# An approximate-matmul residual block on one NeuronCore: indirect writes, weight preparation and a norm placed at other steps

## The chip, the cores and the metric

The kernel runs on one core of a Trainium2 chip. The metric is the device time of one execution in microseconds, taken as the median of several executions. All data is fp32.

## What is computed

The input `x` has 16 samples of 256 channels of 28 x 28 pixels. Each sample is group-normalised (32 groups of 8 channels), goes through two "approximate matmul" 3 x 3 convolutions with a batch norm each, a squeeze-and-excite gate, and two residual additions:

```python
def amm_conv3x3(x, centroids, w_sub, stride=1):
    patches = jax.lax.conv_general_dilated_patches(x, (3, 3), ...)
    p = patches.reshape(B, C, s, Ho * Wo).transpose(0, 3, 1, 2)
    d = jnp.sum(p * p, -1)[..., None] - 2.0 * jnp.einsum('bncs,cks->bnck', p, centroids) + ...
    attn = jax.nn.softmax(-d, axis=-1)
    lut = jnp.einsum('cks,cso->cko', centroids, w_sub)
    out = jnp.einsum('bnck,cko->bno', attn, lut)
...
out = amm_conv3x3(x, centroids1, wsub1)
out = relu(bn_inference(out, ...))
out = amm_conv3x3(out, centroids2, wsub2)
out = se_layer(bn_inference(out, ...), ...)
return x0 + relu(out + x)     # x = group norm of x0
...
```

For every channel and pixel, the 9 patch values are compared with 16 centroids, a softmax over these 16 gives weights, and the weighted centroids times `w_sub` are summed over all 256 channels and 9 taps.

## The kernel before, in words

The program is one long unrolled list. It goes through 32 samples: 16 samples of layer 1 (numbers 0 to 15), then the same 16 of layer 2 (16 to 31). Each sample is four blocks: two halves of the channels (`hh`) by two halves of the image (14 rows, 392 pixels). A block takes two steps, so a sample takes 8 steps and the whole program some 256 and a tail. "Step 6.3" below means step 3 of sample 6, which is number 8 x 6 + 3 = 51 in the code.

The order is written out by hand. `at(cl, sub, f, ...)` (line 843) files a call under the step `cl` and a place `sub` in it; at line 1040 all calls are made in the order of `(cl, sub)`. Every engine then executes its own instructions in just this order. A place in the list is thus a place in each of the queues that the call uses: TensorE (PE), VectorE (DVE), ScalarE (ACT), GpSimd (POOL) and SyncE (SP, which issues most DMAs). An instruction that waits holds up all that is behind it on its engine.

One step of TensorE holds, in this order:

- sub 0.1 and 0.2, `logits` (line 357): patches times centroids, 32 x 32 tiles, 64 records in the trace. They read `pt`, the patches, which SP loads from the DRAM scratch `home1` or `home2` two steps ahead (`patches`, sub 0.5). ACT then makes exponentials (`exps`, line 369).
- in even steps sub 1.3 `num_b` (line 418) and 1.35 `num_a` (line 404): sums of exponentials, and numerators. In odd steps `num_a` alone, at 1.0.
- sub 2.0, `product` (line 486, tile `acc`): the normalised weights `q` times the weight matrices, mostly 18 records of 340 ns. This is the lookup and sum over channels. One of eight products falls in each step; step 6 has a short one.

The softmax's division: DVE makes a reciprocal, spreads it over partitions (`spread`, tiles `rb`), and GpSimd multiplies (`scale_q`, line 467: at sub 1.71 for the ninth tap in even steps, twice at 1.8 in odd steps). The products are arranged in the manner of Strassen's scheme: GpSimd also subtracts whole `q` buffers (`mix`, line 495), so a product may wait for a GpSimd that is late. Mixes stand at sub 2.5 of steps 5 and 7, 1.75 and 2.6 of step 7, and 1.0 of step 2.

Work around this that the change touches:

- `to_home2` (line 549): when a sample of layer 1 is finished, its two channel halves (`o`), each in two shifted copies (`r`), are written to `home2[b]` by indirect DMAs that GpSimd issues. Rows go to places given by an index tile `col`, since layer 2 uses its channels in another order. There are four writes per sample. They go to the same tensor, so each waits until the one before has landed. In sample 0 the order isn't known yet; its output is kept in DRAM (`d_h0`) and written later from a stage buffer (`h0_load`, `h0_put`).
- the order of channels: `rank_make` on DVE, `rank_look` (an indirect read, line 616), `rank_cols`.
- preparation of layer 2's weights during layer 1: `codes_load/put` and `sub_load/put` load centroids and `w_sub` into the stage buffer and scatter their rows by indirect writes (line 629); `prep_wd0` to `prep_wd4` lay out and centre the centroids (`center_sq` on GpSimd, line 259, gives `sq`; `center_add` has a matmul `sqp`, line 264, that reads it, and a DVE add); `prep_cw*` make the matrices of the numerators; `sums_load/put` make sums of weight matrices in five pieces. The stage buffer `st` (tag "pb") exists once, so each of these waits for the one before to be read out.
- `norm_out` (line 532): the batch norm of one quarter of a sample, on ACT. In layer 2 it also sums its output (`accum_out`) for the gate; `se_hidden` (line 752) multiplies these sums on TensorE.
- `gn_mean` (line 295): group statistics of the next input sample.

Of the kernel before, what the change touches and what calls it, by code (L numbers as in the profile page):

```python
# [8 lines left out]
F32 = mybir.dt.float32  # L9
I32 = mybir.dt.int32  # L10
U32 = mybir.dt.uint32
AF = mybir.ActivationFunctionType
# [5 lines left out]
P = 128  # L18
# [7 lines left out]
K = 16  # L26
S = 9
# [40 lines left out]
def kernel(  # L68
# [20 lines left out]
    nc = tc.nc  # L89
    B, C, _ = x.shape  # L90
    NB = C // P
# [4 lines left out]
    small = ctx.enter_context(tc.tile_pool(name="small", bufs=2))  # L96
# [144 lines left out]
    bn = []  # L241
# [53 lines left out]
    def gn_mean(b, k0=0, n=NB):  # L295
        st, mv = gst[b]
        ps = bank("gnp")[:, : 2 * n]
        nc.tensor.matmul(
            ps, lhsT=gmat, rhs=mv[:, k0 : k0 + n].rearrange("p b t -> p (b t)"), start=True, stop=True
        )  # L300
        gm = small.tile([P, NB, 2], F32, name="gn_gm")
        nc.vector.tensor_copy(gm[:, :n].rearrange("p b t -> p (b t)"), ps)
        dv = small.tile([P, NB], F32, name="gn_dv")
        nc.vector.tensor_sub(dv[:, :n], mv[:, k0 : k0 + n, 0], gm[:, :n, 0])
        nc.vector.tensor_mul(dv[:, :n], dv[:, :n], dv[:, :n])
        gst[b, "m"] = gm, dv

# [189 lines left out]
    ys = {}  # L497
# [34 lines left out]
    def norm_out(l, b, o, t, src=None):  # L532
# [5 lines left out]
        else:  # L538
# [4 lines left out]
                accum_out=ys[b, "sum"][:, o, t : t + 1],  # L543
            )

    idx = {}

    def to_home2(b, o, r, src=None):
        nc.gpsimd.indirect_dma_start(
            out=home2[b].rearrange("c u n -> (c u) n"),  # L550
            out_offset=bass.IndirectOffsetOnAxis(ap=idx["col", o, 5 + r][:, 0:1], axis=0),
            in_=(hpads[o] if src is None else src)[:, r : r + HROW], in_offset=None,
        )
# [74 lines left out]
    def scatter(dst, col, o, src):  # L628
        nc.gpsimd.indirect_dma_start(
            out=dst, out_offset=bass.IndirectOffsetOnAxis(ap=idx["col", o, col][:, 0:1], axis=0),  # L630
            in_=src, in_offset=None,
        )

    pw = {}
# [5 lines left out]
    def h0_load(o):  # L640
        nc.sync.dma_start(stage()[:, :NPAD], d_h0[o * P : (o + 1) * P, :])

    def h0_put(o):
        for r in range(2):
            to_home2(0, o, r, pw["st"])

    def codes_load(o):
        st = stage()
        nc.sync.dma_start(st[:, : S * K], sk2[o * P : (o + 1) * P, :])
        nc.sync.dma_start(st[:, 256 : 256 + S * K], ks2[o * P : (o + 1) * P, :])  # L650

    def codes_put(o):
        st = pw["st"]
        scatter(d_sk, 0, o, st[:, : S * K])
        scatter(d_ks, 1, o, st[:, 256 : 256 + S * K])

    def sub_load(o, part):
        n = 4 * C if part < 2 else C
# [93 lines left out]
    def se_hidden(b):  # L752
        ysum = ys[b, "sum"]
        ps = bank("sep")[: 2 * RED, :1]
        n = 0
        for k in range(NB):
            for i in range(2):
                nc.tensor.matmul(  # L758
                    ps, lhsT=w1_sb[:, k, :], rhs=ysum[:, k, i : i + 1],
                    start=(n == 0), stop=(n == 2 * NB - 1),  # L760
                )
                n += 1
        hid = small.tile([2 * RED, 1], F32, name="se_hid")
        nc.scalar.activation(hid, ps, AF.Relu, bias=b1_sb, scale=1.0 / HW)
        se[b] = small.tile([2 * RED, NB], F32, name="se_hh")
        nc.scalar.activation(se[b], halves, AF.Copy, scale=hid)
# [76 lines left out]
    def at(cl, sub, f, *a, **kw):  # L843
        jobs.setdefault((cl, sub), []).append((f, a, kw))
# [20 lines left out]
    for j, u in enumerate(blocks):  # L865
        g = 2 * j
        u["w"] = j
        wide = u["l"] == 1 and u["hh"] == 0
        for p in range(2):
            u["pt", p] = pts[p]  # L870
            at(g + p - NPT, 0.5, patches, u, p, nc.gpsimd if 0 < g + p < 5 else None)
            for q in range(2):
                mm = 2 * p + q
                at(g + p, 0.1 + 0.1 * q, logits, u, mm)
                if wide and mm == 0:
                    at(g, 0.12, wide_copy, u, mm)
                    at(g, 0.9, wide_turn, u, mm)
                    at(g, 0.95, wide_sub, u, mm)
                    at(g + 1, 0.3, wide_back, u, mm)
                    at(g + 1, 0.9, wide_exp, u, mm)  # L880
                else:
                    at(g + p, 0.12 + 0.1 * q, exps, u, mm)
        at(g + 2, 1.3, num_b, u)
        at(g + 2, 1.4, split_b, u)
        at(g + 2, 1.5, join_b, u)
        at(g + 2, 1.6, recip_dve, u)
        at(g + 2, 1.7, spread, u, 4)
        at(g + 2, 1.71, scale_q, u, 4)
        for mm in range(2):
            at(g + 2, 1.35, num_a, u, mm)  # L890
            at(g + 2, 1.45, copy_a, u, mm)
            at(g + 3, 1.8, spread, u, mm)
            at(g + 3, 1.8, scale_q, u, mm)
        for mm in range(2, 4):
            at(*((g + 2, 1.8) if mm == 2 else (g + 3, 0.05)), spread, u, mm)
            at(g + 3, 1.0, num_a, u, mm)
            at(g + 3, 1.1, scale_a, u, mm)

    for l in range(2):
        for b in range(B):  # L900
# [17 lines left out]
            at(g + 10, 0.05, reg_add, l, b, c12, c22, None)  # L918
            at(g + 10, 0.06, reg_add, l, b, c22, c21, None)
            at(g + 11, 0.0, acc_add, l, b, c12, (n, 10))  # L920
            at(g + 11, 1.9, norm_out, l, b, *c12)
            at(g + 11, 1.91, norm_out, l, b, *c22)
            at(g + 12, 0.0, acc_add, l, b, c11, (n, 11))
            at(g + 12, 0.3, norm_out, l, b, *c11)
            at(g + 13, 0.0, acc_add, l, b, c21, (n, 12), op=ALU.subtract)
            at(g + 13, 0.3, norm_out, l, b, *c21)
            if l == 0:
                for o in range(2):
                    if b == 0:
                        at(g + 12 + o, 0.35, rank_score, o)  # L930
                        at(g + 12 + o, 0.6, rank_keep, o)
                        at(g + 12 + 2 * o, 0.65, h0_keep, o)
                    else:
                        for r in range(2):
                            at(g + 12 + o + (o and r), (0.5, 2.9)[r] if o == 0 else (2.4, 2.9)[r], to_home2, b, o, r)
                if b + 1 < B:
                    at(*((g - 1, 2.6) if b else (2, 1.65)), load_x, b + 1)
                    for q in range(NB):
                        at(g + (1 + q if b else 4), 0.3, gn_stats, b + 1, q)
                    at(g + (3 if b else 4), 2.1, gn_mean, b + 1)  # L940
                    at(g + 4, 2.1 if b else 2.2, gn_var, b + 1)
                    for q in range(NB):
                        at(g + 5, 0.9 if b else 0.3, gn_apply, b + 1, q)
                        at(g + 5, 1.9 if b or q else 0.9, to_home1, b + 1, q)
            else:
                last = b == B - 1
                at(*((g + 11, 0.6) if last else (g + 13, 2.6)), load_x, b, last)
                at(g + 13, 2.1, se_hidden, b)
                at(g + 14, 1.05 if last else 2.1, se_gate, b)
                for q in range(NB):  # L950
                    at(*((g + 12, 0.4) if last else (g + 19, 0.9)), finish_norm, b, q)
                    if not last:
                        at(g + 19, 0.91, finish_gate, b, q)
                        at(g + 20, 0.05, finish_sum, b, q)
                        at(g + 20, 0.9, finish_relu, b, q)
                        at(g + 21, 0.05, finish_add, b, q)
                        at(g + 21, 0.06, store, b, q)
                    else:
                        at(g + 14, 1.92, finish_fast, b, q)
                        at(g + 14, 1.92, store, b, q)  # L960
                if b == B - 1:
                    at(g + 11, 0.65, flags)
                    at(g + 12, 2.9, flag_sum)
# [12 lines left out]
    at(14, 0.7, rank_row)  # L976
    for o in range(2):
        at(15 + o, 1.9, rank_make, o)
        at(16 + o, 2.7, rank_look, o)
    for o in range(2):  # L980
        at(18 + o, 2.7, rank_cols, o)
        at(20 + 2 * o, 0.6, h0_load, o)
        at(21 + 2 * o, 2.7, h0_put, o)
        at(24 + 2 * o, 0.6, codes_load, o)
        at(25 + 2 * o, 2.7, codes_put, o)
        for part in range(3):
            c = 28 + 6 * o + 2 * part
            at(c, 0.6, sub_load, o, part)
            at(c + 1, 2.7, sub_put, o, part)
    at(41, 0.6, prep_wd0)  # L990
    at(43, 0.3, prep_wd1)
    for part in range(3):
        at(43 + 2 * part, 1.9, prep_wd2, part)
        at(44 + 2 * part, 1.05, prep_wd3, part)
    at(51, 1.9, prep_wd4)
    at(52, 0.6, prep_cw0)
    at(53, 1.9, prep_cwa)
    for part in range(4):
        at((59, 60, 67, 68)[part], 2.3, prep_cwb, part)
    at(92, 2.3, load_se)  # L1000
    for n in range(5):
        at(70 + 2 * n, 0.6, sums_load, 2 * n)
        at(71 + 2 * n, 2.3, sums_put, 2 * n)
    g = 8 * B
    at(g - 2, 0.4, load_wd, 1, 0)
    at(g, 0.4, load_wd, 1, 1)
# [190 lines left out]
```

## Time and profile before

| | |
|---|---|
| median of 3 runs | 2750.07 us (2749.22 to 2758.3) |
| profiled execution | 2756.05 us |
| its span, first to last instruction | 2754.6 us |
| granted TensorE clock | 0.993 |
| indirect writes to `home2` (line 549) | 64, each 1.0 us of GpSimd |
| 392-column norm of layer 2 (line 541) | 64, median 763 ns, and 250 ns to read the sum |
| subtraction or product of a pair on GpSimd | 128 x 784, 1.86 us |
| layer 2's norm of the input (line 790) | 128 x 784, median 1096 ns |
| landing of a `home2` write after its issue | 3.2 to 8.4 us, median 5.8 |

The profile is of one execution. A line of its groups or timeline gives start and duration in us, engine, line of the code, operation, output and inputs, shape, count, and in brackets the idle time of the engine just before with what ended it. A matmul's end is modelled. A group of matmuls that overlap has a length from its first start to its last end, not a sum.

### The profile page before, as it was taken

To read this page: it belongs to the slowest core of one execution; us is meant where nothing else is said; L and a number is where in the kernel's file an instruction comes from. 1 tells how busy PE (TensorE), PEld (TensorE's weight loads), DVE (VectorE), ACT (ScalarE), POOL (GpSimd) and SP (SyncE) were. 2 spreads that over 40 slices of the span, in tenths; PEclk is the share of its full clock that TensorE was granted. 3 is DMA by queue.
4 is the path that set the end of the run, shared out by engine and by line. 5 is a ranking of instruction groups with operands and counts; after the bars stand their busy time and mean duration, and the time that the engine had idled before them with its cause. 6 is when DMAs were issued, how large, how long until landed. Compare 5 with 4: busy or idle time off the path is not lost.

```text
span 2754.6 us, 87978 instructions
## 1 busy us (share of the span) xinstructions
PE 2684.1 (97%) x37044; PEld 1298.7 (47%) x37044; DVE 1717.0 (62%) x3943; ACT 1461.7 (53%) x3293; POOL 2076.5 (75%) x1425
## 2 busy tenths in 40 slices
PE   5899999999999999999999999999999999999998
PEld 2444444444444444444444444444444444444444
DVE  4765555566655565555477666676666676766674
ACT  3445455444545444555455566665566565566553
POOL 3856787767887667766678687888787779787787
PEclk9999999999999999999999999999999999999999
DMA  9675676655677656655585555545555545555442
GB/s 195 149 141 145 157 188 183 163 118 146 153 184 186 156 120 157 165 157 148 116 184 123 112 117 119 111 100 118 123 122 119 113 101 116 119 124 119 109 106 60
DMA packets 223626, 374.53 MB, mean 136 GB/s; under 512 B 30633, under 2 KB 194009, under 8 KB 223225
## 3 DMA queue, kind: packets, MB, share of 16 engines
q1 hardware_dynamic: 216280, 334.87, 53.7%
q0 software_dynamic: 6944, 33.95, 3.6%
q8 instruction: 296, 4.85, 0.8%
q14 instruction: 106, 0.86, 0.1%
HBM read 288.93 MB, written 79.80 MB: 134 GB/s over the span
## 4 chain that ended last, share of the span: by engine, by line
PE 89%; DMA 3%; POOL 3%; SPq 1%; issue 1%; DVE 1%; ACT 1%; ACTq 0%; POOLq 0%; DVEq 0%
PE acc L486 47%; PE lg L357 17%; PE na L404 12%; PE nb L418 12%; DMA pt<-home 2%; POOL qp L495 2%; DMA home<-xpad 1%; SPq L343 1%; POOL qp L467 1%; SPq L347 1%; DMA row<-in_before 0%; ACT e L369 0%; POOL qo L493 0%; PE sep L758 0%; PE sep L770 0%
## 5 line engine op out<-in xcount | busy, mean ns | idle before, releaser
L369 ACT ACTIVATE e<-lg 128x392 f32<-128x392 f32 x1920 | 779.9, 524 | 795.4 <-PE lg L357 793.5
L495 POOL TENSOR_TENSOR qp<-qp,qp 128x784 f32<-128x784 f32 x512 | 939.0, 1864 | 21.5 <-DVE qp L478 21.5
L486 PE MATMUL acc<-qp,w_S 128*128 128x392 f32 x2048 | 706.6, 495 | 3.9 <-POOL qp L495 3.7
L467 POOL TENSOR_TENSOR qp<-qp,rb 128x784 f32<-128x784 f32 x256 | 470.1, 1857 | 209.4 <-DVE rb L459 201.3
L357 PE MATMUL lg<-pt,wd 32*32 32x392 f32 x16384 | 555.9, 503 | 19.7 <-DMA pt<-home 15.0
L459 DVE STREAM_SHUFFLE rb<-r 128x392 f32<-128x392 f32 x1024 | 550.9, 603 | 0.0
L486 PEld LDWEIGHTS acc<-qp,w_S 128*128 128x128 f32 x2048 | 386.8, 190 | 304.0 <-issue 15.7
L486 PE MATMUL acc<-qp,w_A 128*128 128x392 f32 x1536 | 521.3, 492 | 0.0
L438 DVE SCALAR_TENSOR_TENSOR r<-nb,kst,r 128x392 f32<-128x392 f32 x128 | 79.8, 623 | 570.9 <-ACT r L429 547.0
L404 PE MATMUL na<-e,cwa 64*32 64x392 f32 x8192 | 410.5, 496 | 8.5 <-issue 6.2
L486 PEld LDWEIGHTS acc<-qp,w_A 128*128 128x128 f32 x1536 | 291.8, 190 | 213.8
L418 PE MATMUL nb<-e,cwb 64*32 64x392 f32 x8192 | 374.9, 499 | 2.6 <-issue 2.1
L357 PEld LDWEIGHTS lg<-pt,wd 32*32 32x32 f32 x16384 | 236.3, 103 | 266.8 <-issue 184.7
L444 DVE RECIPROCAL r<-r 128x392 f32<-128x392 f32 x128 | 331.8, 2592 | 0.0
L467 POOL TENSOR_TENSOR qo<-qo,rb 128x392 f32<-128x392 f32 x128 | 131.1, 1024 | 247.8 <-DVE rb L455 247.6
L478 DVE TENSOR_TENSOR qp<-na,rb 128x392 f32<-128x392 f32 x512 | 252.5, 554 | 71.2 <-PE na L404 68.0
L404 PEld LDWEIGHTS na<-e,cwa 64*32 64x32 f32 x8192 | 146.9, 106 | 237.2 <-ACT e L369 119.9
L418 PEld LDWEIGHTS nb<-e,cwb 64*32 64x32 f32 x8192 | 143.8, 108 | 225.3 <-issue 140.8
L472 ACT COPY qp<-na 128x392 f32<-128x392 f32 x512 | 212.4, 513 | 12.0 <-PE na L404 10.2
L429 ACT ACTIVATE r<-nb,kst 128x392 f32<-128x392 f32 x128 | 87.7, 685 | 115.0 <-PE nb L418 111.2
L493 POOL TENSOR_TENSOR qo<-qo,qo 128x392 f32<-128x392 f32 x128 | 130.9, 1023 | 2.2
L375 ACT COPY e<-lg 128x392 f32<-128x392 f32 x128 | 52.9, 500 | 149.8 <-PE lg L357 149.8
(147 smaller groups left out, 1769.7 us busy)
## 6 DMA issues: line engine op xcount, KB each, us to landing
pt<-home SPq DMA_DIRECT2D x768, 209.0 KB
pt<-home SPq DMA_DIRECT2D x756, 104.5 KB
home<-xpad SPq DMA_DIRECT2D x31, 899.0 KB
xt<-in_x SPq DMA_DIRECT2D x30, 784.0 KB
out_dram<-y SPq DMA_DIRECT2D x32, 392.0 KB
w_S<-d_wS SPq DMA_DIRECT2D x4, 576.0 KB
st<-in_wsub SPq DMA_DIRECT2D x4, 512.0 KB
st<-d_wa SPq DMA_DIRECT2D x16, 128.0 KB
```

Source lines behind the costliest of these rows:

```text
L357: nc.tensor.matmul(bk[32 * c : 32 * c + 32, :N].rearrange("p (r w) -> p r w", w=W), lhsT=wts["wd", u["hh"]][32 * i : 32 * i + 32, mm, c, : ...
L369: nc.scalar.activation(eg[:, i, :], bk[:, :N], AF.Exp, scale=2.0)
L404: nc.tensor.matmul(bs[r][32 * i : 32 * i + 32, :N], lhsT=wts["cwa", u["hh"]][64 * r : 64 * r + 64, mm, i, :], rhs=es[64 * r : 64 * r + 64, ...
L418: nc.tensor.matmul(bs[r][32 * i : 32 * i + 32, :N], lhsT=wts["cwb", u["hh"]][64 * r : 64 * r + 64, mm, i, :], rhs=es[64 * r : 64 * r + 64, ...
L444: nc.vector.reciprocal(u["r"], u["r"])
L459: nc.vector.stream_shuffle(rb[:, r, :], u["r"], mask_of(2 * mm + r))
L467: nc.gpsimd.tensor_tensor(q, q, u.pop(("rb", mm)), ALU.mult)
L472: nc.scalar.copy(u["q", 2 * mm + r], bk[:, :N])
L478: nc.vector.tensor_mul(u["q", 2 * mm + r], bk[:, :N], rb[:, r, :])
L486: nc.tensor.matmul(accs[key][:, :N], lhsT=wl[w][:, k, :], rhs=us["q", k], start=first and n == 0, stop=last and n == len(ks) - 1,)
L493: nc.gpsimd.tensor_tensor(out_u["q", 8], in0["q", 8], in1["q", 8], ALU.subtract)
L495: nc.gpsimd.tensor_tensor(pair(out_u, mm), pair(in0, mm), pair(in1, mm), ALU.subtract)
```

## The change

- Layer 1's `to_home2` writes: (o=0, r=0) goes from sub 0.5 to 1.72 of step 12 of its sample's schedule (step 4 of the sample after), behind `scale_q` 4; (o=1, r=0) goes from 2.4 to 1.805 one step later, between the two calls of `scale_q`, for which these are now filed at 1.8 and 1.81. The two with r=1 stay at 2.9.
- `rank_look` for both halves goes to step 17, sub 1.805.
- The writes of sample 0 (`h0_put`) are filed one by one; `codes` start at step 32 instead of 24, `w_sub` at 36 instead of 28, and their writes are filed at 1.77, 1.78, 1.805 or 2.7 instead of always 2.7.
- All preparation after that goes 8 steps later; `prep_wd3` also goes from sub 1.05 to 2.1.
- The five pieces of `sums_load/put` start at 82 and follow every 8 steps, instead of from 70 every 2 steps.
- In layer 2, but for the last sample, four `norm_out` of 392 columns become two `norm_both` of 784, at 0.3 of steps 12 and 13 of the sample's schedule; `se_hidden` has two matmuls instead of four.
- In `gn_mean` one subtraction reads its operand from PSUM instead of the copy.

```diff
-        nc.vector.tensor_sub(dv[:, :n], mv[:, k0 : k0 + n, 0], gm[:, :n, 0])
+        nc.vector.tensor_sub(dv[:, :n], mv[:, k0 : k0 + n, 0], ps.rearrange("p (b t) -> p b t", t=2)[:, :, 0])
...
+    def norm_both(b, o):
+        sc, sh = bn[1]
+        if o == 0:
+            ys[b, "sum"] = small.tile([P, NB, 2], F32, name="ysum")
+        nc.scalar.activation(
+            ys[b, o], ys[b, o], AF.Identity, bias=sh[:, o : o + 1], scale=sc[:, o : o + 1],
+            accum_out=ys[b, "sum"][:, o, 0:1],
+        )
...
+        terms = [(k, i) for k in range(NB) for i in range(2 if b >= B - 1 else 1)]
...
-            at(g + 3, 1.8, spread, u, mm)
-            at(g + 3, 1.8, scale_q, u, mm)
+            at(g + 3, 1.8 + 0.01 * mm, spread, u, mm)
+            at(g + 3, 1.8 + 0.01 * mm, scale_q, u, mm)
...
-            at(g + 11, 1.9, norm_out, l, b, *c12)
-            at(g + 11, 1.91, norm_out, l, b, *c22)
-            at(g + 12, 0.3, norm_out, l, b, *c11)
-            at(g + 13, 0.3, norm_out, l, b, *c21)
+            if l == 0 or b == B - 1:
+                at(g + 11, 1.9, norm_out, l, b, *c12)
+                at(g + 11, 1.91, norm_out, l, b, *c22)
+                at(g + 12, 0.3, norm_out, l, b, *c11)
+                at(g + 13, 0.3, norm_out, l, b, *c21)
+            else:
+                for o in range(NB):
+                    at(g + 12 + o, 0.3, norm_both, b, o)
...
-                            at(g + 12 + o + (o and r), (0.5, 2.9)[r] if o == 0 else (2.4, 2.9)[r], to_home2, b, o, r)
+                            at(g + 12 + o + (o and r), (1.72, 2.9)[r] if o == 0 else (1.805, 2.9)[r], to_home2, b, o, r)
...
-        at(16 + o, 2.7, rank_look, o)
+        at(17, 1.805, rank_look, o)
...
-        at(21 + 2 * o, 2.7, h0_put, o)
-        at(24 + 2 * o, 0.6, codes_load, o)
-        at(25 + 2 * o, 2.7, codes_put, o)
+        for r in range(2):
+            at(*(((21, 1.77), (21, 1.808)), ((23, 2.7), (25, 1.78)))[o][r], h0_put, o, r)
+        at(32 + 2 * o, 0.6, codes_load, o)
+        for i in range(2):
+            at(33 + 2 * o, 1.78 if o == i == 0 else 1.805, codes_put, o, i)
         for part in range(3):
-            c = 28 + 6 * o + 2 * part
+            c = 36 + 6 * o + 2 * part
             at(c, 0.6, sub_load, o, part)
-            at(c + 1, 2.7, sub_put, o, part)
-    at(41, 0.6, prep_wd0)
-    at(43, 0.3, prep_wd1)
+            at(c + 1, (1.77, 2.7, 1.78, 1.805)[(3 * o + part) % 4 if o == 0 else (3, 0, 1)[part]], sub_put, o, part)
+    at(49, 0.6, prep_wd0)
+    at(51, 0.3, prep_wd1)
     for part in range(3):
-        at(43 + 2 * part, 1.9, prep_wd2, part)
-        at(44 + 2 * part, 1.05, prep_wd3, part)
+        at(51 + 2 * part, 1.9, prep_wd2, part)
+        at(52 + 2 * part, 2.1, prep_wd3, part)
...
-        at((59, 60, 67, 68)[part], 2.3, prep_cwb, part)
+        at((67, 68, 75, 76)[part], 2.3, prep_cwb, part)
...
-        at(70 + 2 * n, 0.6, sums_load, 2 * n)
-        at(71 + 2 * n, 2.3, sums_put, 2 * n)
+        at(82 + 8 * n, 0.6, sums_load, 2 * n)
+        at(83 + 8 * n, 2.3, sums_put, 2 * n)
```

## The prediction

> **What bounds the kernel now.** I read the page first: TensorE is busy almost throughout, and the chain that ended last is nearly all TensorE.
>
> ```profile
> PE 2684.1 (97%) x37044; PEld 1298.7 (47%) x37044; DVE 1717.0 (62%) x3943; ACT 1461.7 (53%) x3293; POOL 2076.5 (75%) x1425
> PE 89%; DMA 3%; POOL 3%; SPq 1%; issue 1%; DVE 1%; ACT 1%; ACTq 0%; POOLq 0%; DVEq 0%
> ```
>
> But a busy TensorE need not be at its pace. So I cut the span at the first logits matmul of every sample (8 steps) and asked for these stretches (columns: stretch and length, then busy us of PE, PEld, DVE, ACT, POOL, granted clock, DMA share, GB/s). Samples 3, 6, 13 of layer 1 and 18 of layer 2:
>
> ```profile
> 281.02:370.87 89.85, 87.89 (x1155) 41.27 (x1154) 48.06 (x122) 42.89 (x96) 70.20 (x53) 1.00 0.71 184
> ...
> 541.08:632.44 91.36, 86.30 (x1157) 41.68 (x1157) 56.87 (x131) 42.45 (x96) 64.84 (x46) 0.98 0.62 147
> ...
> 1139.00:1222.09 83.09, 83.09 (x1156) 40.46 (x1155) 48.01 (x123) 42.36 (x96) 59.07 (x43) 1.00 0.59 148
> ...
> 1551.96:1633.99 82.03, 82.03 (x1162) 39.92 (x1161) 55.55 (x120) 48.93 (x110) 66.75 (x41) 1.00 0.53 116
> ```
>
> The same matmuls take 82.03 at best. Layer 2 runs at that pace (82.03 in most samples), so there is nothing to win but work taken from TensorE. Samples 2 to 16 sum to 1278.0 (191.89 to 1469.92), against 15 x 82.03 = 1230.5: 47.5 us over. The change acts there.
>
> Where a late sample loses its time, I read in the timeline, on TensorE and GpSimd together. First step 6 of sample 13, then sample 14's, then layer 2's, then two steps of sample 4, then GpSimd there:
>
> ```profile
> 1204.98 3.29 PE L357 MATMUL lg<-pt,wd 32*32 32x392 f32 x64
> ...
> 1206.05 1.02 POOL L549 DMA_INDIRECT home<-hpad,col  x1 [0.15 <-PE lg L357]
> ```
> ```profile
> 1288.07 3.29 PE L357 MATMUL lg<-pt,wd 32*32 32x392 f32 x64
> ...
> 1289.15 1.03 POOL L549 DMA_INDIRECT home<-hpad,col  x1 [0.16 <-PE lg L357]
> ```
> ```profile
> 1699.86 2.02 PE L357 MATMUL lg<-pt,wd 32*32 32x392 f32 x64
> ```
> ```profile
> 383.06 2.02 PE L357 MATMUL lg<-pt,wd 32*32 32x392 f32 x64
> 385.02 1.64 PE L404 MATMUL na<-e,cwa 64*32 64x392 f32 x32
> 386.58 0.93 PE L486 MATMUL acc<-qo,w_S 128*128 128x392 f32 x2
> 387.35 5.43 PE L486 MATMUL acc<-qp,w_S 128*128 128x392 f32 x16
> 392.71 3.15 PE L357 MATMUL lg<-pt,wd 32*32 32x392 f32 x64
> ```
> ```profile
> 387.15 1.01 POOL L629 DMA_INDIRECT d_wa<-st,col  x1
> ```
>
> 64 logits records take 2.02, but 3.15 to 3.29 when an indirect write is issued 0.6 to 1.1 us after their start. The write at 387.15 lies in a product (L486, "acc") and costs nothing: its step is 9.65. No wait is shown; TensorE is merely slowed, by 1.1 to 1.3 per issue of 1.0. Issued in the na part (line 404, step 5 of sample 13, at 1197.50) it costs nothing either.
>
> **Rule against row.** The Trainium skill, "SBUF — State Buffer", section Who interferes with whom, says TensorE and ScalarE never wait on anyone and that a DMA never contends with a compute engine. By it an issue could not slow logits, and moving issues would win only the queue waits. The rows repeat (samples 3, 4, 10, 12, 13, 14: 3.15 to 3.32), and other placements are clean, so I take the row; the rule makes a rival below.
>
> **A. to_home2 (4 per sample, samples 2 to 16).** The third write (o=1, r=0) moves from sub 2.4, behind both products with rb (scale_q), to between them. In sample 13 scale_q starts at 1202.24 and one takes 1.83, so the issue goes from 1206.05 to about 1204.2-1205.2. Step 6 begins at 1204.98: 0.2 of it still touches logits. The first write moves behind scale_q 4 (ends 1194.19), so to 1194.3-1195.3, the end of the product of step 4; its present 5.11 wait for ACT goes, but is idle GpSimd time, worth nothing itself. Logits excess of step 6 now: samples 3 to 14 sum to 12.7 without sample 5 (its excess is a centering matmul). In samples 8 and 9 the moved cwb pieces (step 4 there: second write at +4.69 instead of +2.16, as samples 7 and 8 show now) keep the third write late: keep 1.8. Residue 11 x 0.2 = 2.2. Samples 15, 16: 1.7 now, 0.4 left. Gain 12.7 - 1.8 - 2.2 + 1.3 = **10**.
>
> The four writes of a sample go to one tensor and wait for each other's landing:
>
> ```profile
> 1436.49 1.01 POOL L549 DMA_INDIRECT home<-hpad,col  x1 [4.50 <-ACT hpad L537]
> ...
> 1443.60 1.01 POOL L549 DMA_INDIRECT home<-hpad,col  x1 [0.97 <-DMA home<-hpad,col]
> ```
>
> The first now follows later, so this chain tightens: issue at -1.1 (from the start of step 5), then the second after gn_var at +2.16 or after landing, then the third at +8.9 or after landing. Landing takes 3.2 to 8.4, median 5.8, in the trace; issued into quiet stretches (1361.41, 280.16, 1453.75) 3.3 to 3.9, at +2.16 mostly 4.7 to 5.8. So 2.8, then 8.6: just in time. The skill's "DMA: Bandwidth & Descriptors", Anatomy of one DMA, fits 2.0 us + bytes/436 GB/s: an estimate of 3.06 for 460 KB, no wait at all. I take the rows, and their upper end as the slower rival.
>
> **B. Writes of ranks, h0, codes and w_sub (16 issues).** Losses now beside them, by step of sample: 2.1 1.1 (na part 2.69 against 1.6), 2.7 1.2, 3.0 1.5 (GpSimd blocked 3.81 by the landing before h0's second write; the mixes come late), 3.2 1.9 (half logits; half pt late, because SP waits for the stage buffer), 3.4 2.1 (two codes), 3.7 1.25, 4.2 1.0, 4.4 0.3, 4.7 1.2: 11.5. After, order and idle places put them at the head of steps 5 or 1 (na or product), or between the scale_q of odd steps, in products; sub 2.7 of step 7 falls at +4.1 of step 1, as w_sub does at 387.15. Left: h0's second write of step 21, fifth in the row, spills into step 22 (0.6, in place of 0.95 there), two w_sub behind the second to_home2 delay the third (0.6 each), the pair at 35 overruns by 0.2. SP's loads go along; behind one SP waits until the stage buffer is read, which costs no pt now at 387 either. Gain **10**.
>
> **C. Centering (prep_wd3).** TensorE stands at
>
> ```profile
> 546.63 0.70 PE L264 MATMUL sqp<-sq,nhalf_sb 128*128 128x256 f32 x2 [3.53 <-POOL sq L259]
> ```
>
> because GpSimd reaches sq only behind its mixes. Step 6.0 is 18.11 against 12.19, 5.9 over; 5.4 1.9; 5.6 0.8. At sub 2.1 the matmul stands behind the product, some 10 us later, with sq long done. Its own 0.65 x 3 stays. Gain 8.6 - 2.0 = **6.5**. The vector add behind it on DVE waits for the product's end, as the next accumulator add does anyway.
>
> **D. Sums of weights.** Pieces now follow every 2 steps in 70 to 79 and meet home1's writes and the pt loads: steps 8.7 1.9, 9.0 1.6, 10.0 1.6 late. After: always step 2 to 3, where the piece at 74/75 costs 0 to 0.2. Five x 0.2 = 1 left. GpSimd's 4 x 0.73 falls into its idle 5.1. SP stands up to some 3 us behind these, before patches with over 10 us of slack. Gain **4**.
>
> **E. Norm of layer 2.** Two ACT instructions of 763 + 250 ns (read of the accumulator) become one of 784 columns: nearest row 1096 ns (L790) + 250. ACT wins 1.4 per sample, but is busy 49 of 82: hidden. In step 4 ACT reaches split_b some 0.35 later; were scale_q 4's slack gone (it has 6 us), that would cost 0.35 x 15 = 5. se_hidden loses 4 of its 8 TensorE records, 0.034 apart: 15 x 0.14 = **2**. The gn_dv operand from PSUM: same 0.16 instruction, 17 times, between -0.1 and +0.1 each, mostly hidden; 0.
>
> **F. Moved only.** wd0 to cwb go one sample later in the same phase: their losses in 6.4 (1.6), 6.7 and 7.0 (2.7) reappear in 7.4 to 8.0. 0, with -3 to +3 unknown.
>
> Sum 10 + 10 + 6.5 + 4 + 2 = **33**, rounded. The profiled execution took 2756.05 (span 2754.6): 2723 there. The runs' median 2750.07 lies 6 lower: 2717.
>
> **Rivals.** (1) The issue isn't what slows logits (a store in flight or the bank order would; for it: the rule, and no wait named). Then A's 10 and most of B's vanish; left are C, D, E and B's queue waits (1.5 + 1.0): 15, so 2735. Against it: clean issues in products. 18%. (2) **Slower**: the landing chain. The third write blocks scale_q 1 and the mixes behind it on GpSimd: issue 1.0 + 1.85 + 1.0 + 1.85 = 5.7 until TensorE's second product operand, wanted at step 6 +6.83, or +8.1 if the logits are slowed as now. The two landings may then last 13.1 together; from 14.9 on it eats the other 23 us (1.8 x 13). At 7.8 + 8.4 = 16.2, the longest seen, 3.1 x 13 = 40 lost: +17, 2767. Against: only such extremes in pairs do it. 8%. (3) Only A fails and moved work collides: within 0.3%, 2747, 4%. Main case 70%, own range 2708 to 2730.
>
> A measurement here tells 0.3% (8 us) from no change. Faster: main and (1), 0.87; same 0.05; slower 0.08. The range takes in (1) and the unknowns of F: 2704 to 2741.
>
> **What would show it.** Right: samples 10 to 14 at about 82.0 to 82.3; logits of step 6 near 2.2; the third indirect write before step 6; no wait of sqp on sq; step 72 and 80 near 12.2. Wrong: waits of home on "DMA home" in GpSimd's list with mixes late, logits still at 3.2 with no issue in them, or layer 2 above 82.0.

## The result, and the profile after

| | before | after |
|---|---|---|
| median | 2750.07 us (2749.22 to 2758.3, 5 runs) | 2732.52 us (2726.74 to 2734.14, 5 runs) |
| profiled execution, its span | 2756.05, 2754.6 us | 2732.52, 2731.0 us |
| ratio of the times | | 0.9926, 95% interval [0.9908, 0.9944] |

The change wins 17.5 us, where 33 were forecast. The page of the changed kernel (engine busy time, then the chain that ended last):

```profile
PE 2663.6 (98%) x36984; PEld 1293.3 (47%) x36984; DVE 1718.3 (63%) x3943; ACT 1445.9 (53%) x3233; POOL 2075.3 (76%) x1425
...
DVE 0%; issue 0%
```

TensorE is still the bound: 2663.6 of 2731.0. The 60 records that have gone are those of `se_hidden` (4 in each of 15 samples). This time the chain breaks off at the last instructions of VectorE, so it says nothing about the rest. The stretches of samples 3, 6, 13 and 18, cut as before (stretch and length, busy us of PE, PEld, DVE, ACT, POOL, granted clock, DMA share, GB/s):

```profile
277.73:359.49 81.76, 81.76 (x1155) 40.36 (x1154) 48.01 (x123) 42.10 (x96) 61.28 (x45) 1.00 0.65 164
529.23:615.31 86.08, 85.06 (x1160) 41.16 (x1159) 53.00 (x127) 42.10 (x96) 64.05 (x48) 1.00 0.61 150
1118.38:1200.41 82.03, 82.03 (x1156) 40.35 (x1155) 48.27 (x123) 42.10 (x96) 62.71 (x48) 1.00 0.65 164
1530.32:1612.24 81.92, 81.92 (x1157) 39.80 (x1157) 55.51 (x120) 48.17 (x106) 66.72 (x41) 1.00 0.53 116
```

Sample 3 has lost all its excess (89.85 before), sample 6 over half of it (91.36), sample 13 one microsecond (83.09), and layer 2 runs at 81.92 instead of 82.03. Sample 13 in the timeline of TensorE and GpSimd, from the end of step 4 to step 6:

```profile
1173.73 1.01 POOL L558 DMA_INDIRECT home<-hpad,col  x1 [0.15 <-issue]
...
1177.38 1.06 POOL L558 DMA_INDIRECT home<-hpad,col  x1 [0.65 <-DMA home<-hpad,col]
...
1183.28 1.02 POOL L558 DMA_INDIRECT home<-hpad,col  x1 [0.40 <-PE acc L486]
1184.34 1.87 POOL L467 TENSOR_TENSOR qp<-qp,rb 128x784 f32<-128x784 f32 x1
1184.38 2.03 PE L357 MATMUL lg<-pt,wd 32*32 32x392 f32 x64
```

The third write now ends before step 6 begins (1184.38), and the logits of that step take 2.03 instead of 3.29. This write of the sample, the second, waits 0.65 for the landing of the first; over the whole profile such waits sum to 18.1 in 16 times, against 2.3 before. TensorE doesn't feel them: what it waits for GpSimd's products `qp` has fallen from 3.7 to 0.9. So far all is as forecast. But 17.5 is not 33. In the list of what TensorE waited for (us in total, times, longest), the wait of `sqp` on GpSimd's `sq`, 3.5 before, is gone. These lines are among those that grew:

```profile
PE na L404 <- issue: 9.0, 6, 4.1
...
PE lg L357 <- DVE hpad L523: 3.5, 4, 1.3
PE nb L418 <- issue: 3.4, 2, 1.8
```

Before, they were 6.2, 1.8 and 2.1 in total. Of the first, 7.5 lie in sample 1, where the change moves nothing. The second holds a new wait of 1.15 at step 4.4. The third is two stalls with no releaser in the trace (nothing is seen that TensorE waited for), at steps 8.0 and 14.0. The last two come back below.

### The profile page after: what moved, and what is told of

Its sections match the earlier page's. It is cut to its first block, busy times and chain, and to the rows that moved or that the text cites. A ratio compares the mean times of both kernels' runs of the same rounds, so it can differ in the third digit from the quotient of the medians.

```text
span 2731.0 us, 87796 instructions
## 1 busy us (share of the span) xinstructions
PE 2663.6 (98%) x36984; PEld 1293.3 (47%) x36984; DVE 1718.3 (63%) x3943; ACT 1445.9 (53%) x3233; POOL 2075.3 (76%) x1425
## 5 line engine op out<-in xcount | busy, mean ns | idle before, releaser
L357 PE MATMUL lg<-pt,wd 32*32 32x392 f32 x16384 | 541.2, 504 | 21.1 <-DMA pt<-home 16.2
```

The lines of the kernel that those rows point to most:

```text
L357: nc.tensor.matmul(bk[32 * c : 32 * c + 32, :N].rearrange("p (r w) -> p r w", w=W), lhsT=wts["wd", u["hh"]][32 * i : 32 * i + 32, mm, c, : ...
```

## The experiments

"The changed kernel" is the kernel after the change. The three groups of runs below were made on three different chips, here 4, 1 and 0 in this order; the chip of the first pair of profiles is not recorded. The changed kernel as it is was run on chips 1 and 0, not on 4. Part B was never put back by itself. Ratios are to runs of the kernel before on the same chip, whose median was 2743.5, 2743.3 and 2743.2 there.

### Does an indirect issue slow the logits?

The first group puts an issue where none was. In each sample of layer 2 but the last, a small indirect read into an unused tile is filed inside the logits of step 6, or in the product of step 5, or, as a control, a plain DMA of GpSimd inside the logits. The fourth kernel files the writes of `to_home2` at their old places.

```diff
+    probe_t = const.tile([P, MAPC], U32, name="probe_t")
+    def probe():
+        nc.gpsimd.indirect_dma_start(
+            out=probe_t, out_offset=None, in_=ids,
+            in_offset=bass.IndirectOffsetOnAxis(ap=idx["col", 0, 0][:, 0:1], axis=0),
+        )
...
+                    at(g + 13, 2.505, probe)
```

(2.505 lies between GpSimd's first `mix` and the next. The product's probe stands at 1.805. The control has `nc.gpsimd.dma_start(probe_t, ids[0:P, :])`.)

> The changed kernel with one more indirect DMA per sample of layer 2 but the last: GpSimd reads 128 rows of 28 bytes by index into a spare tile that nothing reads. It is issued behind the first mix of step 5, so some 0.8 us into the logits of step 6. Theory 'issue' (what slows TensorE is GpSimd's issue of an indirect DMA itself): the 64 logits records of step 6 take about 3.2 us instead of 2.02, each such sample 0.9 to 1.3 us longer than 81.92, 15 samples: 13 to 19 us more than the changed kernel. Rival 'traffic' (the 460 KB that a to_home2 write moves, or the order of PSUM banks in layer 1, is what slows it; this DMA moves 3.5 KB): logits stay at 2.0, within 2 us of the changed kernel.

> The same small indirect DMA, but between the two calls of scale_q in step 5, so inside the product of TensorE. Theory 'issue': 0 to 0.3 us per sample, within 4 us of the changed kernel, although GpSimd does the same extra work and its mixes come 1 us later just the same. Rival 'late mixes' (it is GpSimd's 1 us of delay that counts, not where it lies): as long as the run with the issue inside the logits.

> At the place inside the logits a plain DMA of the same size, also issued by GpSimd, without indices. Theory 'issue' in its wide form (any DMA whose descriptors GpSimd makes slows TensorE's logits): as in the indirect run, logits 2.6 to 3.2 us and 8 to 19 us more. In its narrow form (only the indirect one with its 128 rows read one by one): within 3 us of the changed kernel.

> The changed kernel with the to_home2 writes of samples 1 to 15 back at their old places (0.5 and 2.4). My prediction's part A: 8 to 12 us slower than the changed kernel, with step 6 of samples 10 to 14 back at 9.5 us and its logits at 3.2. Rival 'traffic' or 'bank order': no difference beyond 2 us, since the same writes are made in the same steps, 2 us apart.

| | time | ratio | step 6 of layer 2 |
|---|---|---|---|
| probe in logits | 2725.8 | 0.9943 [0.9921, 0.9964] | 8.70 |
| probe in the product | 2728.73 | 0.9952 [0.9937, 0.9966] | 8.55 |
| plain DMA in logits | 2726.53 | 0.9942 [0.9922, 0.9963] | 8.55 |
| `to_home2` at its old places | 2728.42 | 0.9948 [0.9928, 0.9967] | 8.55 |

Step 6 is 8.55 without a probe. TensorE and GpSimd in the timeline of the kernel with the probe in the logits, sample 20:

```profile
1747.89 2.18 PE L357 MATMUL lg<-pt,wd 32*32 32x392 f32 x64
1748.89 0.99 POOL L567 DMA_INDIRECT probe_t<-in_ids,col  x1
```

The issue stands 1.0 after the start of the logits, where the prediction saw 1.1 to 1.3 lost. Here it costs 0.15. With the writes at their old places, step 6 of samples 10 to 14 takes 8.24, less than in the changed kernel's first profile (8.24 to 8.55). By its steps, part A is worth nothing on this chip; in the whole time, 2728.42 lies within the noise of the three probes.

But the probe is a small read, and in these runs the old third write came 0.3 after the start of the logits and not 1.1. So the second group files the real write, 460 KB, at 2.505, and profiles both kernels once more as they are. It also tests the new loss at step 4.4, for which see further down.

```diff
-at(g + 12 + o + (o and r), (1.72, 2.9)[r] if o == 0 else (1.805, 2.9)[r], to_home2, b, o, r)
+at(g + 12 + o + (o and r), (1.72, 2.9)[r] if o == 0 else (2.505, 2.9)[r], to_home2, b, o, r)
```

> The changed kernel with the third to_home2 write (460 KB) of samples 1 to 15 behind the first mix, so 0.8 to 2 us into the logits of step 6, where the first profile of the kernel before showed logits of 3.2 us. Theory 'issue, but only of a large write' (rows of 3.6 KB under load; the small extra DMA was too light): step 6 at 9.3 to 9.6, 12 to 18 us slower than the changed kernel. Theory 'chip': step 6 at 8.2 to 8.5, within 4 us of it.

> The kernel before, unchanged, profiled on the chip of the experiments. The three runs with an extra DMA showed no slow logits in layer 2 (0.15 us at most), and with the old places of to_home2 the logits of step 6 stayed at 1.95. Theory 'chip' (the slow logits beside an issue belong to the chip or the execution of the first profile): samples 10 to 14 have step 6 at 8.2 to 8.6 here, and their sum of steps is 82.0 or so. Rival 'program' (the kernel before has them wherever it runs, and something else in the change removed them): step 6 at 9.5, logits 3.2, as in the first profile.

> The changed kernel, unchanged, on the same chip. Theory 'chip': its gain here is smaller than the 17.5 us of the first comparison by what the slow logits cost there, 12 to 15 us, ratio 0.9945 to 0.996. Rival 'program': ratio 0.991 to 0.9935 as before.

The kernel with the third write in mid-logits took 2729.33, ratio 0.9948 [0.9931, 0.9966]; the changed kernel 2725.81, 0.9940 [0.9916, 0.9963]; the kernel before, one run, 2737.93. TensorE and GpSimd in step 6 of sample 13, first in the kernel with the write in mid-logits, then in the second profile of the kernel before:

```profile
1178.20 2.03 PE L357 MATMUL lg<-pt,wd 32*32 32x392 f32 x64
...
1179.46 1.02 POOL L558 DMA_INDIRECT home<-hpad,col  x1 [0.16 <-PE lg L357]
```
```profile
1191.42 2.03 PE L357 MATMUL lg<-pt,wd 32*32 32x392 f32 x64
1191.70 1.02 POOL L549 DMA_INDIRECT home<-hpad,col  x1 [0.15 <-PE acc L486]
```

The very write, issued 1.26 into the logits, leaves them at 2.03 in samples 10 and 12 to 14 (2.2 in 11, 15 and 16; 2.2 to 3.0 in 7 to 9, where the kernel with the writes at their old places has up to 3.7). And the kernel before has no slow logits on chip 1, nor on chip 0 (third group): step 6 of samples 10, 12, 13 and 14 takes 8.24 in both, against 9.48 to 9.50 in its first profile. Another sign parts the first profile from these: there the write started 1.07 after the begin of the logits, here 0.28, since VectorE got the numerators `na` of step 5 later, and with it GpSimd its work. VectorE in step 5 of sample 13, in the first profile and in the second:

```profile
1199.08 1.98 DVE L478 TENSOR_TENSOR qp<-na,rb 128x392 f32<-128x392 f32 x4 [1.91 <-PE na L404]
```
```profile
1184.74 1.98 DVE L478 TENSOR_TENSOR qp<-na,rb 128x392 f32<-128x392 f32 x4 [1.13 <-PE na L404]
```

That is 3.74 after the start of step 5 in the first profile and 2.96 in the second, with the sample's second write at +2.16 in both. In samples 7 and 8 of the first profile, where this write stands at +4.69, it is 2.96 too. So in that execution TensorE's results came late beside an issue in the na part as well, where the prediction took it to cost nothing; in the later ones they did not. The slow logits thus belong to the chip or to the executions of the first pair, not to the issue alone. Which of the two it was, these runs don't tell.

The time of the runs doesn't decide here. With the slow logits gone, the changed kernel was expected at a ratio of 0.9945 to 0.996 on chip 1. It came out at 0.9940, just outside that range, but with an interval that covers all of it.

### What the other parts are worth

The third group puts back C, D and E in one kernel. They touch different samples, and so can be read apart by steps.

```diff
-        at(52 + 2 * part, 2.1, prep_wd3, part)
+        at(52 + 2 * part, 1.05, prep_wd3, part)
...
-        at(82 + 8 * n, 0.6, sums_load, 2 * n)
-        at(83 + 8 * n, 2.3, sums_put, 2 * n)
+        at(78 + 2 * n, 0.6, sums_load, 2 * n)
+        at(79 + 2 * n, 2.3, sums_put, 2 * n)
...
-            if l == 0 or b == B - 1:
+            if True:
...
-        terms = [(k, i) for k in range(NB) for i in range(2 if b >= B - 1 else 1)]
+        terms = [(k, i) for k in range(NB) for i in range(2)]
```

> The changed kernel with three of its parts put back, which touch different samples and so can be read apart: prep_wd3 at sub 1.05 (part C), the sums of weights every 2 steps from step 78 (part D), layer 2's norm in four passes and eight records in se_hidden (part E). Theory (the prediction's C, D, E, corrected by the traces): C brings back TensorE's wait on sq; step 7.0 (12.62 in the changed kernel) becomes about 16 to 18, 7.2 and 7.4 may fall a little: +4 to +5.5 us. D: the pieces fall in steps 9.6 to 11.0: steps 9.7, 10.0 up to +1.5 each, +2 to +3 us. E: every sample of layer 2 at 82.04 instead of 81.92, +1.7 us. Together the span is 8 to 10 us longer, ratio 0.997 where the changed kernel has 0.994. Rival (the gain is made by A and B, and C and D only move losses about): layer 2 82.04, step 7.0 below 14, steps of samples 9 to 11 unchanged; ratio at most 0.001 above that of the changed kernel in this comparison.

> The changed kernel as it is, for comparison with the two above on one chip. Theory (places of instruction refills and the state of samples 0 and 1 vary by some us, the rest repeats): step 4.4 15.9 to 16.0, 5.4 13.0, 7.0 12.6, layer 2 at 81.92, ratio 0.9930 to 0.9945. Rival (the gain differs from chip to chip, since the slow logits beside an indirect write were seen in the first pair of profiles alone): ratio outside 0.991 to 0.996.

> The kernel before, one look. If the slow logits belong to the program (an issue inside logits costs 1.1 to 1.3), step 6 of samples 10, 12, 13, 14 is 9.5 and the third indirect write starts 1.0 to 1.1 after its begin. If they belong to the chip or the execution of the first profile, step 6 is 8.24, as in the second look at this kernel, and the write starts 0.3 after its begin.

The kernel with the three parts put back took 2734.98 (2730.05 to 2740.15, 12 runs), 0.9967 [0.9952, 0.9983]; the changed kernel 2725.47, 0.9946 [0.9924, 0.9967]; the kernel before, one run, 2745.24. The parts are worth 9.5 by the medians. By steps, against the changed kernel on the same chip:

- C: steps 6.6, 6.7 and 7.0 take 10.26 + 7.61 + 17.84, against 8.88 + 9.08 + 12.62. That is 5.1, in two kinds, which the next part separates.
- D: steps 9.6, 9.7, 10.0, 10.6 and 11.0 sum to 54.13 against 51.10: 3.0.
- E: a sample of layer 2 takes 82.04 against 81.92: over 14 samples 1.7.

TensorE at step 7.0 of the kernel with the parts put back:

```profile
615.00 2.03 PE L357 MATMUL lg<-pt,wd 32*32 32x392 f32 x64
620.28 0.70 PE L264 MATMUL sqp<-sq,nhalf_sb 128*128 128x256 f32 x2 [3.26 <-POOL sq L259]
620.91 4.56 PE L418 MATMUL nb<-e,cwb 64*32 64x392 f32 x64
```

The wait on `sq` is back, 3.26. But look at the third line: the same 64 records of `nb` elsewhere take 2.86. They lost another 1.7, with no wait.

### The second loss behind a stall: the granted clock

The same spot of the kernel before (step 6.0, where `sqp` waited 3.53), cut into stretches of 3.41 (columns as above; the granted clock stands third from the end):

```profile
544.40:547.80 3.40, 1.17 (x18) 0.63 (x26) 0.42 (x1) 0.89 (x3) 3.40 (x3) 1.00 0.95 221
547.80:551.21 3.41, 3.41 (x51) 1.31 (x40) 0.00 (x0) 0.00 (x0) 3.41 (x4) 0.50 0.58 135
```

After a stretch with TensorE busy for a third of it, the clock is halved for just one stretch, and TensorE loses 1.71. In all 14 profiles of this study the halved spells are one or two times 3.413 us long, in three cases three times, but for the last, which runs into the end of the program. Their starts lie on one grid of 3.413 us for that execution; where the grid begins differs from execution to execution. For samples 0 to 30 I took TensorE's busy share of each stretch of the grid at full clock. A share under 0.40 was followed by half clock all 43 times, one of 0.40 to 0.50 in 12 of 36 times, one of 0.50 to 0.75 in 14 of 134 (step 4.4 below is such a case), and a higher one never. So whether a stall of 2 us costs 1.71 more depends mostly on whether it falls into one stretch or is cut by the grid; what decides between 0.40 and 0.75 is not known. Step 8.0 of the changed kernel shows both. First its third profile (a stall of 2.05 in one stretch, then half clock), then its first, in which the stall lasts 1.79 and the grid cuts 0.32 of it off into the stretch before:

```profile
693.55:696.96 3.41, 1.36 (x38) 0.60 (x34) 0.00 (x0) 0.23 (x1) 3.41 (x3) 1.00 0.77 209
696.96:700.38 3.42, 3.42 (x23) 1.09 (x8) 2.94 (x4) 2.65 (x6) 3.42 (x3) 0.50 0.56 128
```
```profile
701.38:704.79 3.41, 3.09 (x75) 1.08 (x60) 0.00 (x0) 2.50 (x7) 3.41 (x3) 1.00 1.01 261
704.79:708.20 3.41, 1.94 (x36) 0.73 (x36) 0.35 (x1) 1.06 (x2) 3.41 (x3) 1.00 0.75 193
708.20:711.62 3.42, 3.42 (x12) 2.01 (x11) 3.36 (x4) 1.72 (x5) 3.42 (x3) 1.00 0.47 128
```

The Trainium skill, "TensorE: Matmul & The Clock Gate", part The HAM clock gate, describes this: a free-running window of 3413 ns, after an idle one half rate, after a busy one full rate. The traces agree in length and grid, but TensorE need not be idle for a whole window: busy for up to 0.40 of one, it was always halved in the next.

The clock is also in the times of all runs. The span times one minus the granted clock estimates what half clock took from a run. In the kernel before it averages 24.7 us over 14 runs on chip 1 and 25.5 over 17 on chip 0; in the changed kernel 17.3 and 15.0 over 6 runs each. So by this estimate 7 to 10 of the 17.5 won there are clock. And over the 17 runs, from 2732.54 (clock 0.994) to 2757.12 (0.987), the time rises by 0.91 for each us so lost: most of the scatter of one program is half clock.

The stall of step 8.0 itself has no releaser in the trace. TensorE at that place in the changed kernel's third profile:

```profile
690.95 2.85 PE L418 MATMUL nb<-e,cwb 64*32 64x392 f32 x60
695.85 0.52 PE L418 MATMUL nb<-e,cwb 64*32 64x392 f32 x2 [2.05 <-issue]
```

60 of 64 records are done, then nothing for 2.05. A transfer of the instruction queue begins in this step 4.1 to 4.2 after its start, 0.1 to 0.2 before the last matmul ahead of the stall starts, in this profile and in the first. In the second profile of the same kernel that transfer begins at 4.9, and step 8.0 takes 12.18, with no stall. Such gaps, of 0.8 to 4.3, are in all the profiles of the two kernels; some places return (step 7.0 in all three of the kernel before, 1.2 to 1.7), others differ from one execution to the next. That TensorE waited for its instructions there is likely; no run tested it.

### The new loss at step 4.4

Two writes of codes (step 35 of the code) now stand between the two `scale_q` of one step. The changed kernel's first profile, GpSimd, VectorE and TensorE:

```profile
401.73 1.00 POOL L638 DMA_INDIRECT d_sk<-st,col  x1 [0.15 <-issue]
403.04 0.96 POOL L638 DMA_INDIRECT d_ks<-st,col  x1 [0.30 <-issue]
...
403.78 2.14 DVE L305 TENSOR_TENSOR gn_dv<-gn_dv 128x2 f32<-128x2 f32 x1
404.02 1.86 POOL L467 TENSOR_TENSOR qp<-qp,rb 128x784 f32<-128x784 f32 x1
405.84 0.55 DVE L523 TENSOR_TENSOR hpad<-acc,hpad 128x392 f32<-128x392 f32 x1
406.54 0.86 PE L357 MATMUL lg<-pt,wd 32*32 32x392 f32 x8 [1.15 <-DVE hpad L523]
407.33 4.56 PE L418 MATMUL nb<-e,cwb 64*32 64x392 f32 x64
```

The second `scale_q` comes some 2 late. A square of 128 x 2 numbers on VectorE (L305), which takes 0.16 at least and 0.30 in the median of its 17 times, lasts 2.14 beside this `scale_q`, which takes its usual 1.86. The accumulator add behind it is late, TensorE stands for 1.15, and half clock follows (`nb` 4.56). Step 4.4 takes 15.96 instead of 12.33, where the prediction put the overrun at 0.2. In two kernels one write, and then also the `w_sub` write of step 43, was filed ahead of the first `scale_q`:

```diff
-            at(33 + 2 * o, 1.78 if o == i == 0 else 1.805, codes_put, o, i)
+            at(33 + 2 * o, 1.78 if i == 0 else 1.805, codes_put, o, i)
...
-            at(c + 1, (1.77, 2.7, 1.78, 1.805)[(3 * o + part) % 4 if o == 0 else (3, 0, 1)[part]], sub_put, o, part)
+            at(c + 1, (1.77, 2.7, 1.78, 1.805)[(3 * o + part) % 4 if o == 0 else (2, 0, 1)[part]], sub_put, o, part)
```

> The changed kernel with one of the two code writes of step 35 taken from between the calls of scale_q and filed at 1.78, ahead of both. Theory 'lock' (the pair makes the second scale_q 2 us later, into the stretch where DVE squares gn_dv, and the two block each other: 2.14 us for a DVE instruction of 0.16, then late logits): step 4.4 falls from 14.3 to 16.0 to about 12.4 to 12.8, 1.5 to 3.5 us less in all. Rival (the write filed earlier falls into logits or delays the first scale_q): step 4.3 or 4.4 no shorter.

> The changed kernel with one code write of step 35 and the w_sub write of step 43 filed at 1.78 instead of 1.805, so ahead of the first scale_q and not between the two. Theory (a write between the scale_q's pushes the second scale_q, 1.85 us long, into the vector engine's square of gn_dv[...]): step 4.4 12.9 to 13.1 instead of 16, and step 5.4 12.3 to 12.4 instead of 13.0; together 3.5 us off, ratio about 0.0013 below the changed kernel's. Rival (the number of issues between two products decides, wherever they stand): 4.4 about 16, or 13 with the loss moved into 4.3 or 4.5; 5.4 stays 13.0; no gain.

Step 4.4 falls from 15.97 (chip 1) and 14.27 (chip 0) to 13.02 in both, and step 5.4 in the second from 13.01 to 12.33. The second kernel did as expected; for the first 12.4 to 12.8 had been expected, a small miss. VectorE in the second kernel:

```profile
401.80 0.89 DVE L305 TENSOR_TENSOR gn_dv<-gn_dv 128x2 f32<-128x2 f32 x1
```

The square still meets the `scale_q`, but only its last 0.9, and TensorE doesn't wait. In the whole time the gain can't be told: 2726.0, 0.9929 [0.9904, 0.9955] (changed kernel on that chip 0.9940), and 2725.42, 0.9940 [0.9920, 0.9960] (0.9946). On chip 0 the changed kernel itself had only 14.27 in step 4.4, since no half clock followed, so that 1.25 was left to win there and not 2.95. Neither version measurably beats the change.

## Why the prediction came out as it did

With half clock counted apart, three pairs of profiles of the two kernels can be summed by terms. Each number is the loss before less the loss after, in us, against the steady length of each step (12.19, 9.65, 12.32, 9.76, 12.33, 9.65, 8.24, 7.61 for steps 0 to 7), with half the length of each halved spell taken out into rows of its own. B goes to step 5.3 before and 6.3 after, C from there to 7.0.

| term | forecast | first pair | chip 1 | chip 0 |
|---|---|---|---|---|
| A: step 6 of samples 3 to 16 | 10 | 8.2 | -0.6 | -0.7 |
| B: steps of ranks, h0, codes, `w_sub` | 10 | 6.7 | 1.5 | 2.1 |
| C: steps of `prep_wd0` to `wd4` | 6.5 | 2.1 | 3.2 | 3.3 |
| D and F: the steps behind, to sample 15 | 4 + 0 | 1.9 | 6.9 | 5.6 |
| E: samples 17 to 30 | 2 | 2.4 | 0.9 | 1.5 |
| half clock in samples 2 to 30 | not named | 1.7 | 0.0 | 8.5 |
| half clock before and behind these | not named | 1.5 | 6.3 | 7.3 |
| samples 0, 1, 31 and the start | 0 | -1.1 | 0.1 | -4.2 |
| sum before rounding (sample 16 adds 0.1 at most) | 33 | 23.5 | 18.1 | 23.4 |

The medians of runs give 17.5, 17.5 and 17.7, with intervals of 5 to 6 to either side. The sums of single pairs of profiles scatter, since each profile has its own stalls and half clock. In samples 0, 1 and 31 the change moves no call.

In the first pair, the one that the forecast was made for, A did what it was to do. There the 33 falls short by 4.4 in C, 3.3 in B, 2.1 in D and F and 1.8 in A. On the other two chips A is gone as well, and most of B.

- **A fell on the other chips.** The step that failed is "The rows repeat ..., and other placements are clean, so I take the row". They did repeat, but all in one execution, which can't tell what belongs to a program from what belongs to that execution. The Trainium skill's rule ("SBUF — State Buffer", Who interferes with whom), which was set aside, held on three chips: 0.15 for a probe, 0 to 0.2 for the real write. In the first pair the row held instead.
- **B** was mis-sized for the same reason, as far as the pairs of profiles show. Its list of losses rested on the first profile. In the group's steps the kernel before lost 15.1 there, but 6.8 and 5.8 on the other chips: steps 3.7 and 4.7, listed at 1.25 and 1.2, take the steady 7.61 there. What is won there too lies at step 3.0, where GpSimd stands for the landing before h0's second write (4.39 in the third profile) and the mixes come late. That place cost 1.5, 4.6 and 6.1 in the three profiles, half clock included, and nothing after. Against it stands step 4.4, 1.9 lost, with half clock 3.6 in two of the three, for 0.2 forecast: that GpSimd's lateness reaches TensorE by way of VectorE wasn't in the working.
- **C**: the mechanism was right (no wait on `sq` after; back when undone), the size was not. "5.9 over" at step 6.0 was a wait of 3.5, 1.7 of half clock, and the matmul itself. And the move has a price that was set at nothing: "The vector add behind it on DVE waits for the product's end, as the next accumulator add does anyway". At step 6.7 of the changed kernel eight records of logits wait 0.74 for that add, and the step takes 9.09 instead of 7.61.
- **D** and **E** hold, at 3.0 for 4 and 1.7 for 2 in the kernel that undoes them. D doesn't clear its place, though: in the kernel before, TensorE waits for a DMA ahead of the logits of step 9.0 (1.8 to 3.1), in the changed one ahead of those of 10.0 (1.3 to 2.1). No run tested why. The ACT pass of 784 columns hid as forecast.
- **F**: "0, with -3 to +3 unknown" is not refuted; the table can't tell F from D. The losses went along (7.4 at 13.8 was 6.4 at 14.0 to 14.2; 8.6 at 9.9 to 10.5 was 7.6 at 8.8 to 8.9), and stalls without a releaser come and go at 8.0 and 14.0.
- **Rivals.** The landing chain (rival 2) didn't form. In samples 12 to 14 the third write waits 0.4 to 1.8 and starts in the last 1.1 of step 5 or just as step 6 begins. Rival 1, "The issue isn't what slows logits", with 15 left, gave the better account on the other chips: its 15 for C, D, E and B's waits stands against 12.4 and 12.5 in the rows B to E of chips 1 and 0. That its 2735 is also nearer to 2732.5 than the forecast's 2717 is luck, since in that pair A did win 8.2. The main case was the likelier by its rows and is the one that failed; the range held because it reached to the rival.
- **Left out**: half clock. The windows quoted in the prediction showed 0.98 for sample 6, and the working passed over it. Two more items of its lists are half clock, the 1.1 at step 2.1 and the 1.6 at 9.0; the stretches of the kernel before there are:

```profile
209.88:213.29 3.41, 3.41 (x34) 1.27 (x19) 2.94 (x7) 0.37 (x1) 0.00 (x0) 0.50 0.59 125
803.80:807.21 3.41, 3.41 (x63) 0.89 (x40) 0.00 (x0) 2.87 (x8) 2.27 (x2) 0.50 0.77 154
```

Half clock makes 8.4 of 21.7 us in the mean of the three pairs. Only 3.4 of that lie in samples 2 to 30, where fewer stalls can mean fewer halved spells. Most of the rest lies in samples 0 and 1, where no call moves; there the kernel before had 8.5 to 10.2 of half clock, the changed one and its variants 1.7 to 12. That part looks like chance.

Open: why the logits of the first pair were slow beside an issue, what each write of B is worth, how much of the half clock the change itself removes, and what TensorE waits for in the gaps without a releaser.

## What to carry to other kernels

A loss that repeats within one profile may still be that execution's own. Before a forecast rests on it, it takes a second execution, best on another chip; where a rule speaks against the row, keep the rival's price at full weight. Price a stall of the bounding engine with what follows it: here a wait of 2 or 3 us often cost 1.7 more, by where it fell in the clock's grid. And when two instructions of a slow engine are pushed apart, look at which small instruction of another engine now runs beside the second one.

## What the runs showed of the hardware

TensorE's half clock comes in quanta of 3.413 us on a grid whose start changes with the execution, costs 1.71 a piece, and follows stretches in which TensorE is busy for less than 0.40, and some that are busier, up to 0.75. The two kernels had 10 to 26 us of it in a profile, 4 to 6 of them in the tail. The same program thus scatters without any change in its order: 17 runs of the kernel before lay within 24.6 us, 0.91 for each us of half clock. And a VectorE instruction of 128 x 2 numbers lasted 2.14 instead of 0.16 to 0.30 beside a GpSimd multiplication.
